# Layer 3 with values projected ahead of the attention, chunk ends in 32x32 blocks on VectorE, output written by columns

## The chip, the cores and the metric

The kernel runs on one core of a Trainium2 chip. The metric is the device time of one execution in microseconds. Another execution, recorded by the hardware profiler, gives the trace from which all durations below come. Lines such as L1281 are lines of the kernel before.

## The reference, cut to what matters

Four attention layers follow each other on four images of 64x64 pixels with 64 channels, all in f32. Only layer 3 changes:

```python
h = group_norm(x, gamma, beta)                    # 8 groups
q = h @ wq + bq;  k = h @ wk + bk;  v = h @ wv + bv
attn = softmax(q k^T / 8) over all 4096 pixels    # (4096, 4096) for each image
proj = (attn v) @ wp + bp
return h + proj
```

Each row of `attn` sums to 1. So `(attn v) @ wp + bp` equals both `(attn h) @ (wv wp) + b` and `attn (h @ (wv wp) + b)`, with b = bv wp + bp. The kernel before computes the first form, the changed kernel the second. The product wv wp lies twice on the diagonal of the 128x128 constant `wv3`, and b in `bv3`.

## The kernel before

An image is held as 128 partitions (two halves of the pixel columns, with 64 channels each) by S = 2048 pixels. Queries are cut into NC = 4 chunks of 512 columns (each for both halves), keys into NB = 32 blocks. A unit u is one chunk with one key block, a step is two units, and a layer takes 64 steps for an image. `attention` (L1231) is shared by layers 2 and 3:

- `first(u)` (L1241): four 64x64 matmuls of 512 columns (L1246) write the scores into a PSUM tile `s`. ScalarE writes their exp to `p` (L1251). VectorE adds `p` to `zacc` (L1257), for the even unit of a step at once, for the odd one at the end of the step, over the list `later`.
- `then(u)`, two steps later: four 64x64 matmuls add `v` times `p` into two PSUM accumulators (L1281).
- When a chunk's keys are through, ScalarE copies one accumulator and VectorE adds the other (L1290, L1291) to give `o`, 128 rows of (half, channel) by 512 pixels. Before that VectorE has turned `zacc` in 32x32 blocks and reduced it to `zsums` (L1265, L1269).
- Two steps later comes `turn(c)` (L1300). In layer 3 four 128x128 matmuls multiply 128 columns of `o` each by `wv3` (L1309), which also turns them, so that pixels are partitions. Four matmuls with `lanes`, a 128x32 constant, sum `zsums` over the lanes (L1229). VectorE copies the sums, takes reciprocals and multiplies (L1312, L1313, L1315).
- Two steps after that comes `last` (L1506). VectorE adds the residual `hb` (L1508), and SyncE issues four DMAs of 64 KB whose rows are the 64 channels of a pixel (L1511).

`before3` (L1443) prepares layer 3 of the next image in the background of the attention that runs: the group norm, the queries (`project`, L884), then sixteen 128x128 transposes of h (L1490) in two groups of eight, each copied by ScalarE to `hT` (L1491), and two adds of the bias on VectorE that give `hb` (L1494). `hT` is the `v` of the attention.

The order of the work is written by hand. `step` (L809) emits, for its two units, `first` for both, `then` for the earlier one, one piece of work from a background generator or the list `urgent` (where `MID` is asked for), then the second `then`, then what lies in `later`. All engines take their instructions in this order. `background(0.6, ...)` gives such a place six times in ten. There are two `s` tiles in PSUM (of two banks each), taken in turn by everything that asks, so a background piece or a `turn` takes one of the two between the scores of two steps. There are 14 `p` tiles, four accumulators, two tiles each of `o` and `turned`, and 13 tiles of 128x2048 in SBUF.

The last chunk of the last image ends in `final` (L1513) instead: in two halves, with a check that all softmax sums were in range (`rest_in_range`, `count_bad`; the result `bad` decides whether a general path runs afterwards). `read_flag` puts a load of `bad` into the queues of all engines (L1826).

Of the kernel before, what the change touches and what calls it, by code (L numbers as in the profile page):

```python
# [8 lines left out]
FP = mybir.dt.float32  # L9
I32 = mybir.dt.int32  # L10
AF = mybir.ActivationFunctionType
ALU = mybir.AluOpType
AX = mybir.AxisListType
# [584 lines left out]
def fast_path(tc: tile.TileContext, a: dict, out: bass.AP, bad, read_flag):  # L598
# [56 lines left out]
    def ctile(shape, name):  # L655
        return const.tile(shape, FP, tag=name, name=name)
# [54 lines left out]
    make_identity(nc, ident)  # L711
    ones = ctile([P, P], "ones")
    nc.gpsimd.memset(ones, 1.0)
    lanes = ctile([P, 32], "lanes")
    nc.vector.tensor_reduce(lanes, ident.rearrange("p (a j) -> p j a", j=32), AX.X, ALU.add)

    def twice(dst, src):
        for i in range(2):
# [26 lines left out]
    rows(gamma0, a["L0_conv_gamma"])  # L745


    NCHECK = B * (NB + 2 + 2 * NC * 8)
    all_z, all_r = ctile([P, NCHECK], "all_z"), ctile([P, NCHECK], "all_r")
    checks = [0]  # L750

# [472 lines left out]
        st["done1"] = True  # L1224


    def add_quarters(z, sums):
        for r in range(4):
            nc.tensor.matmul(z[quarter(r), :], lanes, sums[:, r, :, :], start=True, stop=True)  # L1229

    def attention(st, turned_by, arranged, last, not_before, name, final=None):  # L1231

# [38 lines left out]
        def then(u, within=None):  # L1273
            c, j = divmod(u, NB)
            if j == 0:
                accs[c] = [acc_tile() for _ in range(2)]
            p = ps.pop(u)
            for cols in parts(within, j in (0, NB - 1)):
                for e in range(2):
                    for i in range(2):  # L1280
                        nc.tensor.matmul(  # L1281
                            accs[c][e][half(i), cols], v[half(e), j, :], p[half(e), chunk(i)][:, cols],
                            start=(j == 0), stop=(j == NB - 1),
                        )
            if c == NC - 1 and j == NB - 1 and final is not None:
                final(accs.pop(c), by_query(zsums.pop(c)))
            elif j == NB - 1:
                o = os[c] = o_tile("o")
                acc = accs.pop(c)
                nc.scalar.copy(o, acc[0])  # L1290
                nc.vector.tensor_tensor(o, o, acc[1], ALU.add)  # L1291
                urgent.append((now[0] + 2, lambda: turn(c)))
                urgent.append((now[0] + 4, lambda: last(c, os.pop(c))))
                if c == NC - 1:
                    urgent.append((now[0] + 4, lambda: st.update({name: True})))

        def by_query(sums):
            return sums.rearrange("p (i n r) -> p r n i", i=2, n=4)

        def turn(c):  # L1300


            s = s_tile()
            o, z = s[:, 0:512], s[:, 512 : 512 + 2 * 4]
            for n in range(4):
                if turned_by is ident:
                    nc.tensor.transpose(o[:, ds(n * P, P)], os[c][:, ds(n * P, P)], ident)  # L1307
                else:
                    nc.tensor.matmul(o[:, ds(n * P, P)], os[c][:, ds(n * P, P)], turned_by, start=True, stop=True)  # L1309
            add_quarters(z, by_query(zsums.pop(c)))  # L1310
            z_columns, r_columns = check_columns(2 * 4)
            nc.vector.tensor_copy(z_columns, z)  # L1312
            nc.vector.reciprocal(r_columns, z_columns)  # L1313
            t = os[c] = o_p.tile([P, 2 * 4, C], FP, tag="turned", name="turned")
            nc.vector.tensor_tensor(  # L1315
                t.rearrange(arranged, n=4), o.rearrange("p (n i f) -> p n i f", n=4, i=2),
                r_columns.rearrange("p (n i) -> p n i", n=4).unsqueeze(3).to_broadcast([P, 4, 2, C]), ALU.mult,
            )

        start = now[0]  # L1320
        for t in range(pairs):
# [101 lines left out]
    def layer2(st, not_before):  # L1423
        xv = st["x"].rearrange("p (h g e n) -> p e g n h", h=H, e=2, n=4)

        def last(c, t):
            t = t.rearrange("p (i n) h -> p i n h", i=2)
            s = s_tile()
            for e in range(2):
                for i in range(2):  # L1430
                    nc.tensor.matmul(
                        s[half(i), ds(e * 512, 256)], wp2[half(e), :], t[half(e), i, :, :], start=True, stop=True
                    )
            for e in range(2):
                x_out = xv[:, e, c, :, :]
                nc.vector.scalar_tensor_tensor(
                    x_out, s[:, ds(e * 512, 256)].rearrange("p (n h) -> p n h", h=H), bp2, x_out, ALU.add, ALU.add
                )

        return attention(st, ident, "p (n i) f -> p n i f", last, not_before, "done2")  # L1440


    def before3(on, st):  # L1443
# [38 lines left out]
        st["k"] = h, swapped("h_swapped", h)  # L1482
        st["q"] = x_tile("q")
        yield from project(on, st["q"], blocks[3][0], h, blocks[3][1])
        hT, hb = x_tile("hT"), x_tile("hb")
        for g in range(2):
            yield MID
            s = s_tile()
            for i in range(8):
                nc.tensor.transpose(s[:, ds(i * P, P)], h[:, ds((g * 8 + i) * P, P)], ident)  # L1490
            nc.scalar.copy(hT[:, wide(g)], s)  # L1491
        for g in range(2):
            yield MID
            nc.vector.tensor_tensor(  # L1494
                hb[:, wide(g)].rearrange("p (j f) -> p j f", f=C), hT[:, wide(g)].rearrange("p (j f) -> p j f", f=C),
                bv3.unsqueeze(1).to_broadcast([P, 16, C]), ALU.add,
            )
        st["v"], st["x"] = hT.rearrange("p (j f) -> p j f", f=C), hb

    def layer3(st, not_before):  # L1500


        hb = st.pop("x").rearrange("p (k i f) -> p k i f", i=2, f=C)
        dst = tokens(out[st["b"]])

        def last(c, t):  # L1506
            ks, i = slice(c // 2 * 8, c // 2 * 8 + 8), c % 2
            nc.vector.tensor_tensor(t, t, hb[:, ks, i, :], ALU.add)  # L1508
            for r in range(4):
                queue = nc.scalar if c == NC - 1 and st["b"] == B - 1 and r % 2 else nc.sync  # L1510
                queue.dma_start(dst[r, :, ks, i, :], t[r * W2 : (r + 1) * W2, :, :])  # L1511

        def final(acc, sums):  # L1513

            z = acc_tile()[:, 0:8]
            add_quarters(z, sums)
            z_columns, r_columns = check_columns(8)
            nc.vector.tensor_copy(z_columns, z)
            nc.vector.reciprocal(r_columns, z_columns)
            rest_in_range(z_columns, r_columns)  # L1520
            r_columns = r_columns.rearrange("p (n i) -> p n i", n=4)
            t = o_p.tile([P, 2 * 4, C], FP, tag="turned", name="turned")
            ks = slice((NC - 1) // 2 * 8, (NC - 1) // 2 * 8 + 8)
            turned = []
            for m in range(2):
                o, cols = o_tile("o")[:, 0:256], slice(m * 256, m * 256 + 256)
                nc.scalar.copy(o, acc[0][:, cols])
                nc.vector.tensor_tensor(o, o, acc[1][:, cols], ALU.add)
                s = s_tile()[:, 0:256]
                for n in range(2):  # L1530
                    nc.tensor.matmul(s[:, ds(n * P, P)], o[:, ds(n * P, P)], wv3, start=True, stop=True)
                turned.append(s)
            set_bad = count_bad()
            for m, s in enumerate(turned):
                n = slice(2 * m, 2 * m + 2)
                part = t.rearrange("p (i n) f -> p n i f", n=4)[:, n, :, :]
                nc.vector.tensor_tensor(
                    part, s.rearrange("p (n i f) -> p n i f", n=2, i=2),
                    r_columns[:, n, :].unsqueeze(3).to_broadcast([P, 2, 2, C]), ALU.mult,
                )  # L1540
                nc.vector.tensor_tensor(
                    part, part, hb[:, ks, (NC - 1) % 2, :].rearrange("p (i n) f -> p n i f", n=4)[:, n, :, :], ALU.add
                )
                if m == 0:
                    set_bad()
            flag.append(read_flag())
            for r in range(4):
                queue = nc.scalar if r % 2 else nc.sync
                queue.dma_start(dst[r, :, ks, (NC - 1) % 2, :], t[r * W2 : (r + 1) * W2, :, :])

        return attention(
            st, wv3, "p (i n) f -> p n i f", last, not_before, "done3", final if st["b"] == B - 1 else None
        )


    def alone(*phases):
# [229 lines left out]
    drain()  # L1786


    count = 2 * 4
    in_range, in_range_r, least = ctile([P, count + 2], "in_range"), ctile([P, count], "in_range_r"), ctile([P, 1], "least")  # L1790

    def most_in_range():
# [75 lines left out]
```

## Time and profile before

| what | value |
|---|---|
| median of 3 runs | 2986.95 us (2986.86 to 2987.16) |
| the profiled execution | 2984.41 us |
| its span, first to last instruction | 2982.6 us |
| granted TensorE clock | 0.999 |
| TensorE (PE) busy | 2957.3 us |
| ScalarE (ACT) busy | 1932.2 us |
| VectorE (DVE) busy | 1799.4 us |
| GpSimd (POOL) busy | 34.0 us |
| DMA | 25.79 MB, mean 9 GB/s |

The span lies 1.8 us inside the profiled execution's own time. An f32 matmul is recorded as two instructions, an f32 transpose as one. Lists of instructions show the start and the duration in us, the engine, the line, the operation, the output and inputs, the tile of the array (64\*64 is a quarter of it), the shape, and how many were merged into the row; square brackets show how long the engine had been idle, and for whom it waited. In rows by group, the two numbers behind the bar are the busy time of the group in us and the mean of one in ns.

### The profile page before, as it was taken

How to read it: one execution, taken by the hardware profiler on the slowest of the kernel's cores; microseconds unless marked ns; L12 is line 12 of the kernel's file. 1: busy time of each engine (PE TensorE's matmuls, PEld its weight loads, DVE VectorE, ACT ScalarE, POOL GpSimd, SP SyncE). 2: the span in 40 equal slices, each digit the busy share in tenths (PEclk: the TensorE clock that was granted, in tenths of full speed). 3: DMA queues.
4: the chain of work that ended last, by engine and by line, in shares of the span. 5: the costliest groups of instructions: out<-in, count | busy, mean ns of one | idle time of the engine just before them, and what ended most of it. 6: DMA issues, size and time to landing. Idle time of an engine off the chain costs nothing.

```text
span 2982.6 us, 64616 instructions
## 1 busy us (share of the span) xinstructions
PE 2957.3 (99%) x28485; PEld 1125.8 (38%) x28485; DVE 1799.4 (60%) x2038; ACT 1932.2 (65%) x2777; POOL 34.0 (1%) x32
## 2 busy tenths in 40 slices
PE   9999999999999999999999999999999999999998
PEld 3333233333344433444443333333343334333333
DVE  2211742588721078862027887777877777877777
ACT  6877777665578866567876655555555655555554
POOL 0000000000000000000000000000000000000000
PEclk9999999999999999999999999999999999999999
DMA  2020000000001000000000000000000000000000
GB/s 37 2 30 5 1 2 15 5 1 15 2 1 29 1 5 2 15 1 16 1 1 5 1 16 1 19 5 9 5 19 8 15 1 2 19 5 5 9 5 10
DMA packets 54177, 25.79 MB, mean 9 GB/s; under 512 B 51968, under 2 KB 51968, under 8 KB 52480
## 3 DMA queue, kind: packets, MB, share of 16 engines
q1 hardware_dynamic: 52176, 21.17, 3.9%
q8 instruction: 225, 3.69, 0.5%
q10 hardware_dynamic: 1712, 0.41, 0.1%
q14 instruction: 64, 0.52, 0.1%
HBM read 4.79 MB, written 4.19 MB: 3 GB/s over the span
## 4 chain that ended last, share of the span: by engine, by line
PE 98%; ACT 1%; DVE 1%; issue 0%; DMA 0%; ACTq 0%; DVEq 0%
PE acc L1281 30%; PE s L1246 30%; PE s L987 15%; PE acc L1018 15%; PE s L1111 2%; PE acc L1137 2%; ACT p L1117 1%; PE s L1309 1%; PE s L1137 1%; PE s L903 1%; PE s L1393 0%; PE s L884 0%; PE s L1307 0%; PE s L1490 0%; PE s L1413 0%; PE s L1172 0%
## 5 line engine op out<-in xcount | busy, mean ns | idle before, releaser
L1251 ACT ACTIVATE p<-s 128x1024 f32<-128x1024 f32 x1024 | 994.4, 1022 | 706.4 <-PE s L1246 698.3
L1257 DVE TENSOR_TENSOR zacc<-zacc,p 128x1024 f32<-128x1024 f32 x960 | 1173.8, 1223 | 352.3 <-ACT p L1251 311.5
L1281 PE MATMUL acc<-p,v 64*64 64x512 f32 (+1 forms) x4480 | 517.8, 556 | 0.0
L1018 PE MATMUL acc<-p,vs 64*64 64x512 f32 (+1 forms) x4224 | 512.4, 578 | 0.5 <-ACT vs L1007 0.5
L997 ACT ACTIVATE p<-s 128x1024 f32<-128x1024 f32 x480 | 486.9, 1015 | 34.7 <-PE s L987 15.9
L1281 PE MATMUL acc<-p,hT 64*64 64x512 f32 x4096 | 494.2, 590 | 0.0
L1246 PE MATMUL s<-q,k 64*64 64x512 f32 x2048 | 490.5, 590 | 1.7 <-ACT p L1117 1.7
L987 PE MATMUL s<-xT,q 64*64 64x512 f32 x2048 | 487.9, 591 | 2.5 <-DVE v L904 0.6
L987 PE MATMUL s<-xT,q_swapped 64*64 64x512 f32 x2048 | 488.6, 591 | 0.7 <-DVE o L1146 0.7
L1246 PE MATMUL s<-q,xT 64*64 64x512 f32 x2048 | 486.9, 589 | 0.0
L1246 PE MATMUL s<-q,h_swapped 64*64 64x512 f32 x2048 | 479.3, 589 | 0.0
L1246 PE MATMUL s<-q,k_swapped 64*64 64x512 f32 x2048 | 477.5, 590 | 0.0
L999 DVE TENSOR_REDUCE all_z<-z 128x1 f32<-128x4 f32 x128 | 20.1, 157 | 629.1 <-ACT p L997 628.8
L1281 PEld LDWEIGHTS acc<-p,v 64*64 64x64 f32 x4480 | 175.4, 133 | 295.0 <-issue 292.6
L1018 PEld LDWEIGHTS acc<-p,vs 64*64 64x64 f32 x4224 | 178.7, 133 | 269.2 <-issue 205.5
L1007 ACT ACTIVATE vs<-v,all_r 64x64 f32<-64x64 f32 x512 | 176.7, 345 | 143.4 <-PE acc L1018 71.1
L1281 PEld LDWEIGHTS acc<-p,hT 64*64 64x64 f32 x4096 | 156.7, 133 | 263.8 <-issue 263.1
L987 PEld LDWEIGHTS s<-xT,q_swapped 64*64 64x64 f32 x2048 | 146.1, 133 | 144.0 <-issue 113.7
L987 PEld LDWEIGHTS s<-xT,q 64*64 64x64 f32 x2048 | 147.2, 133 | 135.1 <-issue 105.8
L1246 PEld LDWEIGHTS s<-q,h_swapped 64*64 64x64 f32 x2048 | 144.0, 133 | 141.2 <-issue 135.6
L1246 PEld LDWEIGHTS s<-q,k_swapped 64*64 64x64 f32 x2048 | 144.4, 133 | 139.8 <-issue 98.1
L1246 PEld LDWEIGHTS s<-q,xT 64*64 64x64 f32 x2048 | 143.4, 133 | 140.0 <-issue 137.7
(232 smaller groups left out, 1593.5 us busy)
## 6 DMA issues: line engine op xcount, KB each, us to landing
k_swapped<-k SPq DMA_DIRECT2D x8, 512.0 KB, 5.3
h_swapped<-xT SPq DMA_DIRECT2D x8, 512.0 KB, 5.5
out_dram<-turned SPq DMA_DIRECT2D x62, 64.0 KB, 1.9
xin<-in_x_dram SPq DMA_DIRECT2D x12, 256.0 KB, 6.4
q_swapped<-q SPq DMA_DIRECT2D x6, 512.0 KB, 6.0
pg<-pg SPq DMA_DIRECT2D x8, 128.0 KB, 2.3
xin<-in_x_dram SPq DMA_DIRECT2D x12, 64.0 KB, 2.4
xin<-in_x_dram ACTq DMA_DIRECT2D x4, 64.0 KB, 2.7
```

What stands on the lines that cost most here:

```text
L903: nc.tensor.matmul(s[:, ds(k * P, P)], rhs[:, ds((g * 8 + k) * P, P)], w, start=True, stop=True)
L987: nc.tensor.matmul(s[half(e), chunk(i)], queries(m, i, e), k[half(i), chunk(c)], start=True, stop=True)
L997: nc.scalar.activation(p, s, AF.Exp, accum_out=z)
L1007: nc.scalar.activation(vs[half(e), :], v[half(e), m, :], AF.Copy, scale=rz[half(e), m : m + 1])
L1018: nc.tensor.matmul(acc[c][half(i), cols], vs[half(e), :], ps[2 * t + n][half(e), chunk(i)][:, cols], start=(m == 0 and e == 0), stop=(m == ...
L1111: nc.tensor.matmul(ss[e][half(m), chunk(i)], pgs[0 if e == d else 1][r, ds(n * P + m * C, C)], th[r, chunk(i ^ j)], start=True, stop=True,)
L1117: nc.scalar.activation(pk[e], ss[e], AF.Exp)
L1137: nc.tensor.matmul(acc[quarter(q), :], g[:, k, :], ps[j, k][q // 2][:, chunk(q % 2)], start=(k == 0 or not bank), stop=(k == NK - 1 or not ...
L1246: nc.tensor.matmul(s[half(e), chunk(i)], k[(j + i) % 2][half(i), ds(j // 2 * P + e * C, C)], q[half(i), chunk(c)], start=True, stop=True,)
L1251: nc.scalar.activation(p, s, AF.Exp)
L1257: add = lambda: nc.vector.tensor_tensor(zaccs[c], p0, p, ALU.add)
L1281: nc.tensor.matmul(accs[c][e][half(i), cols], v[half(e), j, :], p[half(e), chunk(i)][:, cols], start=(j == 0), stop=(j == NB - 1),)
```

## The change

In layer 3 the values are projected in the background, and the end of a chunk is reshaped by VectorE's 32x32 block transpose, not by TensorE. `values` (L897), which layer 0 uses too, takes the place of the transposes of h:

```python
def values(v, w, rhs, bias):
    for g in range(2):
        yield MID
        s = s_tile()
        for k in range(8):
            nc.tensor.matmul(s[:, ds(k * P, P)], rhs[:, ds((g * 8 + k) * P, P)], w, start=True, stop=True)
        nc.vector.tensor_tensor(v[...], s.rearrange(...), bias..., ALU.add)
```

`turn` becomes an argument of `attention`. Layer 2's `turn` does what it did (in its matmuls `lanes[:, 0:32]`). `lanes` is twice as wide, by one more copy at the start. In layer 3:

```diff
@@ before3
-        hT, hb = x_tile("hT"), x_tile("hb")
-        for g in range(2):
-            yield MID
-            s = s_tile()
-            for i in range(8):
-                nc.tensor.transpose(s[:, ds(i * P, P)], h[:, ds((g * 8 + i) * P, P)], ident)
-            nc.scalar.copy(hT[:, wide(g)], s)
-        for g in range(2):
-            yield MID
-            nc.vector.tensor_tensor(hb..., hT..., bv3..., ALU.add)
+        st["v"] = x_tile("v").rearrange("p (j f) -> p j f", f=C)
+        yield from values(st["v"], wv3, h, bv3)
@@ layer3
+        h = st.pop("x"), st["k"][1]
+        dst = out[st["b"]].rearrange("(j e b) (i w) (q f) -> j e b i w q f", e=2, b=16, i=2, q=2)
+        def sums(zsums):
+            s = s_tile()
+            for k in range(2):
+                for i in range(2):
+                    nc.tensor.matmul(
+                        s[half(i), ds(k * 512, 16)], lanes[half(k), :], zsums[half(k), i * 16 : i * 16 + 16],
+                        start=True, stop=True,
+                    )
+            z_columns, r_columns = check_columns(16)
+            nc.vector.tensor_reduce(z_columns, s.rearrange("p (k b) -> p b k", k=2)[:, 0:16, :], AX.X, ALU.add)
+            nc.vector.reciprocal(r_columns, z_columns)
+            return z_columns, r_columns
+        def residual(c):
+            t = o_tile("residual")
+            for e in range(2):
+                nc.vector.transpose(t[half(e), :], h[0 if e == c % 2 else 1][half(e), chunk(c // 2 * 2 + e)])
+            return t
+        def divide(t, r):
+            nc.vector.tensor_tensor(blocked(t), blocked(t), r.unsqueeze(2).to_broadcast([P, n, 32]), ALU.mult)
+        def store(c, t, rows, queues):
+            for n in range(4):
+                e, q = divmod(n, 2)
+                queues[n % len(queues)](dst[c // 2, e, rows, c % 2, :, q, :].rearrange("b w f -> w b f"), ...)
+        def turn(o, zsums):
+            t = o_tile("turned")
+            r = sums(zsums)[1]
+            nc.vector.transpose(t, o)
+            divide(t, r)
+            return t
         def last(c, t):
-            nc.vector.tensor_tensor(t, t, hb[:, ks, i, :], ALU.add)
-            for r in range(4):
-                queue.dma_start(dst[r, :, ks, i, :], t[r * W2 : (r + 1) * W2, :, :])
+            nc.vector.tensor_tensor(t, t, residual(c), ALU.add)
+            store(c, t, slice(0, 16), [nc.sync.dma_start])
```

The DMAs' rows are thus 32 channels of a pixel (128 bytes). There are still four of 64 KB for a chunk. `final` now reads, with `kept[0]` the residual of the last chunk, formed eight steps before the layer's end:

```python
def final(acc, zsums):
    z_columns, r_columns = sums(zsums)
    rest_in_range(z_columns, r_columns)
    t = o_tile("turned")
    for m in range(2):
        o, rows, cols = o_tile("o")[:, 0:256], slice(m * 8, m * 8 + 8), slice(m * 256, m * 256 + 256)
        nc.scalar.copy(o, acc[0][:, cols])
        nc.vector.tensor_tensor(o, o, acc[1][:, cols], ALU.add)
        nc.vector.transpose(t[:, cols], o)
        if m == 0:
            set_bad = count_bad()
        divide(t[:, cols], r_columns[:, rows])
        nc.vector.tensor_tensor(t[:, cols], t[:, cols], kept[0][:, cols], ALU.add)
        if m == 0:
            store(NC - 1, t, rows, [nc.sync.dma_start])
            set_bad()
            flag.append(read_flag())
    store(NC - 1, t, slice(8, 16), [nc.sync.dma_start, nc.scalar.dma_start])
```

Before, `read_flag` stood behind the arithmetic of both halves and ahead of the four DMAs.

## The prediction

> **What bounds the kernel now.** I read the page's busy shares and the chain that ended last first.
>
> ```profile
> PE 2957.3 (99%) x28485; PEld 1125.8 (38%) x28485; DVE 1799.4 (60%) x2038; ACT 1932.2 (65%) x2777; POOL 34.0 (1%) x32
> ...
> PE 98%; ACT 1%; DVE 1%; issue 0%; DMA 0%; ACTq 0%; DVEq 0%
> ```
>
> TensorE is busy for 99% of the span and carries 98% of the chain. So a matmul that goes shortens the kernel, provided that no wait comes in its place; work on other engines counts only where TensorE waits for it, or after its last matmul. Next I read TensorE's list over a chunk end of layer 3, from the first row of one group L1281 to the first of the next.
>
> ```profile
> 1885.68 1.90 PE L1281 MATMUL acc<-p,hT 64*64 64x512 f32 x16
> ...
> 1889.12 1.04 PE L1281 MATMUL acc<-p,hT 64*64 64x512 f32 x8
> 1890.09 1.16 PE L1309 MATMUL s<-wv,o 128*128 128x128 f32 x8
> 1891.17 0.25 PE L1229 MATMUL s<-zsums,lanes 128*32 128x8 f32 x8
> 1891.35 1.09 PE L1281 MATMUL acc<-p,hT 64*64 64x512 f32 x8
> ...
> 1893.98 1.90 PE L1281 MATMUL acc<-p,hT 64*64 64x512 f32 x16
> ```
>
> A plain step takes 1889.12 - 1885.68 = 3.44 us; over the whole of layer 3 it is 3.43 or 3.44. The step with a `turn` takes 1893.98 - 1889.12 = 4.86. A chunk end thus costs TensorE 1.43 us: 1.08 from L1309's start to L1229's, 0.18 for the sums, and 0.17 more than the plain 0.86 on either side, where the tile of the array changes. Then the two kinds of background piece that are exchanged, the transposes of h and, in layer 0's preparation, the projection of values:
>
> ```profile
> 1909.43 1.04 PE L1281 MATMUL acc<-p,hT 64*64 64x512 f32 x8
> 1910.40 1.09 PE L1490 MATMUL s<-ident,xT 128*128 128x128 f32 x8
> ...
> 1914.05 1.90 PE L1281 MATMUL acc<-p,hT 64*64 64x512 f32 x16
> ```
>
> ```profile
> 735.06 1.07 PE L1281 MATMUL acc<-p,v 64*64 64x512 f32 x8
> 736.06 2.05 PE L903 MATMUL s<-wv,xT 128*128 128x128 f32 x16
> ...
> 740.66 1.04 PE L1281 MATMUL acc<-p,v 64*64 64x512 f32 x8
> ```
>
> Steps of 4.62 and 5.60: eight transposes cost 1.19 us, eight f32 matmuls of that shape 2.17.
>
> **1. The matmuls of the chunk ends go: -18.5 us.** L1309 has 120 rows, eight to a `turn`, so there are 15 turns (the sixteenth is in `final`). Each loses 1.43 us and gets the new sums, eight instructions of 64x64 with 16 columns, which no row shows. From below they are streaming alone: L1281's eight of 512 columns take 0.86, so 16 columns take 0.03. From above: layer 2's `turn`, four transposes and the same L1229, lengthens its step by 0.93 (4.36); eight transposes take 1911.42 - 1910.40 = 1.02, so half of that leaves 0.42 for sums with the changes of tile. I take 0.20, near L1229's own 0.18 (as many instructions, nearly as few columns), with no change of tile. 15 x (1.43 - 0.20) = 18.5; bounds 15 x 1.01 = 15.2 and 15 x 1.40 = 21.0.
>
> [...]
>
> **2. Values for transposes: +7.8 us.** Two groups for each of four images, 8 x (2.17 - 1.19) = 7.8. ScalarE's copies L1491 (1.01 us) go; VectorE's adds move from SBUF to PSUM and now set the tile `s` free. That add takes 1.23 us (L904). The next step wants this tile 1.72 us after the matmuls (the second half of L1281 and one unit of scores), so it hides while VectorE is less than about 0.4 us late; in the list for layer 0 it waits for TensorE, not TensorE for it. Bounds: 7.0, and 11 if half of the eight are late by one `zacc` add (1.22 - 0.4 = 0.8 each).
>
> **3. VectorE gets 1.9 us more for each chunk end, hidden but for one place: +0.6 us.** Now it spends 0.17 + 0.20 + 0.69 + 0.68 = 1.74 (L1312, L1313, L1315, L1508). Then: reduce 0.19, reciprocal 0.20, transpose 0.62, divide 0.69, two residual transposes, add 0.69. The transpose's row is
>
> ```profile
> L1265 DVE STREAM_TRANSPOSE p<-zacc 128x1024 f32<-128x1024 f32 x32 | 39.8, 1245 | 2.7
> ```
>
> so 512 columns take 0.62. For 64 partitions I take the same 0.62 (if only elements counted, 0.31). Sum 3.63. In a plain step its list shows it idle for 0.88 us, waiting for the exp (L1251), so 1.9 us is worked off in two steps. The odd unit's `zacc` add and its successors queue behind it and come up to 2 us late; they hold only `p` tiles, of which there are 14 for two a step. The sums' tile `s` comes free after the reduce, about a microsecond before it is wanted. TensorE would wait where a background piece that VectorE evicts follows in the step right after `last`. In the order of the program there is one such place, with layer 2's values:
>
> ```profile
> 2189.39 1.23 DVE L1257 TENSOR_TENSOR zacc<-zacc,p 128x1024 f32<-128x1024 f32 x1 [0.41 <-ACT p L1251]
> 2190.53 0.68 DVE L1508 TENSOR_TENSOR turned<-turned,hb 128x512 f32<-128x512 f32 x1
> 2191.13 1.22 DVE L1257 TENSOR_TENSOR zacc<-zacc,p 128x1024 f32<-128x1024 f32 x1
> ```
>
> With 1.93 instead of 0.68, that odd add ends at 2193.8, the next even one at 2195.0, and the evictions L1418 (1.29 together) at 2196.3, where the tile is wanted at about 2195.7: 0.6 us. Bounds 0 and 3 (five such waits, if VectorE runs later than I reckon).
>
> **4. The end, after the last matmul: +1.3 us.** `read_flag` moves ahead of the second half, and the load stands in every queue:
>
> ```profile
> L1826 ACTq TENSOR_LOAD <-bad x1: 472/472/472, 2975.8 to 2975.8; - x1
> ...
> L1826 DVEq TENSOR_LOAD <-bad x1: 539/539/539, 2976.1 to 2976.1; - x1
> ```
>
> ScalarE's second copy and VectorE's second half now wait behind it. From the reciprocal's end at 2973.64 (unmoved): add 0.35, transpose 0.33, `least` (waiting for POOL) until 2974.52, divide 0.42, add 0.43, `bad` 0.13: 2975.5. The load: 2976.0. Copy 0.38, add 0.43, transpose 0.35, divide 0.42, add 0.43: 2978.0, where L1541 now ends at 2976.52: +1.5. SyncE's four DMAs of the first half (about 0.4 each) and its load are over by 2977.4, and hidden. The last DMAs carry half the bytes in as many pieces as now. Their 1024 pieces keep the DMA engines busy for some 1.65 us (2977.4 to 2979.05); half the size takes 0.83 to 1.65. I take 0.2 off: +1.3. Bounds 0.7 and 2.5 (the load as long as two of its rows).
>
> [...]
>
> **At nothing:** the copy of `lanes` at the start (VectorE is idle for 2.20 us before L728; else 0.2); `kept` and the longer range check in the last steps, 1.9 us against 0.88 idle in each of eight steps; the sixteen DMA issues a layer, behind which SyncE only has `h_swapped`, wanted many steps later. An issue takes 0.46 us; were it twice that, SyncE would be busy 4 us in a chunk of 56.
>
> **Sum:** -18.5 + 7.8 + 0.6 + 1.3 = -8.8 us. The profiled execution's 2984.41 becomes 2975.6 (its span 2973.8). It lies 2.5 us under the median of the runs, so from 2986.95 I forecast **2978.2 us**.
>
> **Rivals.** (a) *VectorE becomes the wait, and the kernel is slower.* Its 1.9 us a chunk end would come back as a late release of a tile `s`. If all of it reached TensorE, it would be 15 x 1.9 = 28 us, so 2978.2 + 28 = 3006; it turns the sign from 0.6 us a chunk end on. For it: background evictions do hold TensorE now and then (the step at 2177.79 is 0.22 too long, behind L1398). Against it: the 0.88 idle in each step, and few background pieces near chunk ends. 6%. (b) *The small sums cost what they cost now*, 0.42 with the change of tile: 15 x 0.22 = 3.3 less, 2981.5. For it: eight instructions with their weight loads have a floor, as L1229 shows with 8 columns. Against it: they need no other tile. 14%. (c) *The values' evictions or the end come out at their upper bounds:* +3.2 or +1.2, together 2982.6. 9%. (d) That the change doesn't do what it says: the built program's order has the 16 groups L1309 gone, 16 of 64x16 sums in place of the four-quarter ones, and nothing else moved on TensorE; under 1%.
>
> **The numbers.** The forecast with small deviations, 2975.5 to 2980.5, has 70%. The lower bounds together, -21.0 + 7.0 + 0 + 0.7 = -13.3, give 2973.7; that all fall together is unlikely, and the range stops at 2975.0, with some 5% below it. The high end takes in (b) and (c): 2983.0, with (a) and little else above it. Some 0.2% (6 us) is what a measurement can tell from no change, so faster means under 2981.0: the forecast and part of (b), 77%. Within it: the rest of (b), (c) and a little of (a), 18%. Slower: 5%.
>
> **What would show it.** In TensorE's list a chunk end's step of about 3.63 us, and a step with values of 5.6; the step two after 2190 lengthened by half a microsecond; the last VectorE add's end 5.4 us, not 3.9, behind the end of the last L1281. Wrong it would be if steps of the turn were followed by steps over 3.44 us, with TensorE or its weight loads waiting for VectorE, or if the sums took over 0.4 us.

## The result and the profile after

| what | before | after |
|---|---|---|
| median of 8 runs each | 2986.94 us (2986.23 to 2987.24) | 2977.85 us (2976.6 to 2978.7) |
| the profiled execution | 2984.41 us | 2978.09 us |
| its span | 2982.6 us | 2976.3 us |
| first score matmul of layer 0 begins | 9.91 | 12.83 |
| from there to the end of the last `then` matmul | 2962.68 | 2951.46 |
| from there to the end of the span | 10.02 | 12.01 |

The ratio of the times is 0.9969, with a 95% interval of 0.9958 to 0.998. The changed kernel is 9.1 us faster; 8.8 was forecast. In the changed kernel the scores are L1243, the `then` matmuls L1278, the sums L1493, the values L904, the residual's transposes L1508, the add of `last` L1530, and the load of `bad` L1830.

The page, its first line and the chain by engine:

```profile
PE 2948.0 (99%) x28421; PEld 1126.3 (38%) x28421; DVE 1832.9 (62%) x2088; ACT 1924.7 (65%) x2769; POOL 34.1 (1%) x32
...
PE 97%; ACT 1%; DVE 1%; SPq 0%; issue 0%; DMA 0%; ACTq 0%; DVEq 0%
```

VectorE has 33.5 us more work, TensorE 9.3 less, and TensorE still carries the chain. TensorE's list over a chunk end of layer 3:

```profile
1894.14 1.04 PE L1278 MATMUL acc<-p,v 64*64 64x512 f32 x8
1895.00 0.26 PE L1493 MATMUL s<-zsums,lanes 64*64 64x16 f32 x8
1895.09 1.07 PE L1278 MATMUL acc<-p,v 64*64 64x512 f32 x8
...
1897.69 1.90 PE L1278 MATMUL acc<-p,v 64*64 64x512 f32 x16
```

The four matmuls L1309 are gone. From the first row to the last it is 3.55 us, where it was 4.86, against 3.43 for a plain step. So the sums cost 0.12 us: the next group begins 0.09 behind them, while their own rows last 0.26 beside their neighbours. The same list over values:

```profile
1913.14 1.04 PE L1278 MATMUL acc<-p,v 64*64 64x512 f32 x8
1914.11 2.05 PE L904 MATMUL s<-wv,xT 128*128 128x128 f32 x16
...
1918.72 1.47 PE L1278 MATMUL acc<-p,v 64*64 64x512 f32 x12
```

From the first row to the last it is 5.58 us; with transposes it was 4.62. Taking TensorE's whole list step by step, from one group of scores to the next, in both kernels, only three things differ by more than a tenth of a microsecond, apart from the very first step (0.2, part of the start):

| steps | before | after | together |
|---|---|---|---|
| 15 chunk ends of layer 3 | 4.86 (once 5.09) | 3.55 (once 3.74) | -19.7 us |
| 8 with the background transposes, now values | 4.62 (twice 4.65) | 5.58 (twice 5.61) | +7.7 us |
| two steps after the chunk end at 2178 (at 2186.2 and 2194.0) | 3.43 | 3.53 and 4.11 | +0.8 us |

The sum, -11.2, is that of the first table. With +2.0 at the end that is -9.2, the difference of the medians to a tenth. The +2.0 is that of one pair of executions; ends scatter by more than a microsecond (table of ends below). The profiled executions differ by less, 6.3, because this one reached its first scores 2.9 us later; that part belongs to neither kernel (last section).

### The profile page after: what moved, and what is told of

Same layout as the page of the kernel before. It is cut to its first block, busy times and chain, and to the rows that moved or that the text cites. A ratio compares the mean times of both kernels' runs of the same rounds, so it can differ in the third digit from the quotient of the medians.

```text
span 2976.3 us, 64497 instructions
## 1 busy us (share of the span) xinstructions
PE 2948.0 (99%) x28421; PEld 1126.3 (38%) x28421; DVE 1832.9 (62%) x2088; ACT 1924.7 (65%) x2769; POOL 34.1 (1%) x32
## 4 chain that ended last, share of the span: by engine, by line
PE 97%; ACT 1%; DVE 1%; SPq 0%; issue 0%; DMA 0%; ACTq 0%; DVEq 0%
PE acc L1278 30%; PE s L1243 29%; PE acc L1019 15%; PE s L988 15%; PE s L1112 2%; PE acc L1138 2%; PE s L904 1%; ACT p L1118 1%; PE s L1138 1%; PE s L1367 0%; PE s L885 0%; PE s L1405 0%; PE s L1084 0%; PE s L1173 0%; PE s L1424 0%
## 5 line engine op out<-in xcount | busy, mean ns | idle before, releaser
L1248 ACT ACTIVATE p<-s 128x1024 f32<-128x1024 f32 x1024 | 994.4, 1022 | 709.2 <-PE s L1243 702.7
L1278 PE MATMUL acc<-p,v 64*64 64x512 f32 (+1 forms) x8576 | 1011.0, 572 | 0.0
L1278 PEld LDWEIGHTS acc<-p,v 64*64 64x64 f32 x8576 | 335.1, 133 | 555.2 <-issue 551.5
L998 ACT ACTIVATE p<-s 128x1024 f32<-128x1024 f32 x480 | 487.3, 1015 | 34.6 <-PE s L988 15.8
L1243 PE MATMUL s<-q,k 64*64 64x512 f32 x2048 | 490.5, 590 | 1.7 <-ACT p L1118 1.7
L1243 PE MATMUL s<-q,xT 64*64 64x512 f32 x2048 | 487.7, 589 | 0.0
L1243 PE MATMUL s<-q,h_swapped 64*64 64x512 f32 x2048 | 479.6, 589 | 0.4 <-DVE v L1392 0.4
L1243 PE MATMUL s<-q,k_swapped 64*64 64x512 f32 x2048 | 477.3, 590 | 0.0
L1243 PEld LDWEIGHTS s<-q,h_swapped 64*64 64x64 f32 x2048 | 144.5, 133 | 141.4 <-issue 131.0
L1243 PEld LDWEIGHTS s<-q,k_swapped 64*64 64x64 f32 x2048 | 144.9, 133 | 139.1 <-issue 96.7
L1243 PEld LDWEIGHTS s<-q,xT 64*64 64x64 f32 x2048 | 144.4, 133 | 139.1 <-issue 132.9
L1243 PEld LDWEIGHTS s<-q,k 64*64 64x64 f32 x2048 | 144.9, 133 | 118.8 <-issue 103.1
L1118 ACT ACTIVATE p<-s 128x1024 f32<-128x1024 f32 x128 | 124.2, 1022 | 80.8 <-PE s L1112 80.8
```

Of the source, the lines that this page charges most:

```text
L998: nc.scalar.activation(p, s, AF.Exp, accum_out=z)
L1118: nc.scalar.activation(pk[e], ss[e], AF.Exp)
L1243: nc.tensor.matmul(s[half(e), chunk(i)], k[(j + i) % 2][half(i), ds(j // 2 * P + e * C, C)], q[half(i), chunk(c)], start=True, stop=True,)
L1248: nc.scalar.activation(p, s, AF.Exp)
L1278: nc.tensor.matmul(accs[c][e][half(i), cols], v[half(e), j, :], p[half(e), chunk(i)][:, cols], start=(j == 0), stop=(j == NB - 1),)
```

## The experiments

Nine new kernels were run, one of them twice, and both kernels once more. "Profiled once" is one profiled execution; its time contains the chance of the start, so the steps in its trace are compared. The others were timed in several runs besides, and the number of these is given. Each is a change to the changed kernel unless it says otherwise.

**The sums in the tile of 128 rows** (profiled once).

```diff
-            for k in range(2):
-                for i in range(2):
-                    nc.tensor.matmul(s[half(i), ds(k * 512, 16)], lanes[half(k), :], zsums[half(k), i * 16 : i * 16 + 16], ...)
+            for i in range(2):
+                nc.tensor.matmul(s[half(i), 0:16], lanes, zsums[:, i * 16 : i * 16 + 16], start=True, stop=True)
...
-            nc.vector.tensor_reduce(z_columns, s.rearrange("p (k b) -> p b k", k=2)[:, 0:16, :], AX.X, ALU.add)
+            nc.vector.tensor_copy(z_columns, s[:, 0:16])
```

> The changed kernel with its softmax sums in two matmuls of all 128 rows (128x64 tiles, 4 instructions) in place of four of 64 rows (8 instructions); the result is the same. Theory (a change of the array's tile costs TensorE something of itself): the step of a chunk end gets longer than the 3.55 us it has, to some 3.7, for the 0.17 us that the change of tile cost in the kernel before; 15 steps, +2 us. Rival (only instructions count): half the instructions, so 3.49, -1 us in all.

Measured: 14 of the 15 chunk ends take 3.82 to 3.85 us, the one of 3.74 takes 4.05: +0.27 to +0.30 each, +4.1 in all. The direction is that of the theory, the size twice what was expected; the rival fell. From TensorE's list of this kernel:

```profile
1894.08 1.04 PE L1278 MATMUL acc<-p,v 64*64 64x512 f32 x8
1895.05 0.29 PE L1492 MATMUL s<-zsums,lanes 128*64 128x16 f32 x4
...
1897.90 1.90 PE L1278 MATMUL acc<-p,v 64*64 64x512 f32 x16
```

Half as many instructions cost 0.39 us instead of 0.12: 0.97 passes before they start (0.86 with their neighbours' tile). The price of such small sums is in the other tile, 0.27 us for going there and back. The run doesn't tell a price of the change itself from sums that don't run beside their neighbours because their tile covers both halves of the rows.

**Values alone, in the kernel before** (profiled once): the projected values come in, the chunk ends keep TensorE's shape with transposes in place of L1309.

```diff
-        hT, hb = x_tile("hT"), x_tile("hb")
...
+        hT = x_tile("hT")
+        st["v"], st["x"] = hT.rearrange("p (j f) -> p j f", f=C), hT
+        yield from values(st["v"], wv3, h, bv3)
...
-                    nc.tensor.matmul(s[:, ds(n * P, P)], o[:, ds(n * P, P)], wv3, start=True, stop=True)
+                    nc.tensor.transpose(s[:, ds(n * P, P)], o[:, ds(n * P, P)], ident)
```

> The kernel before with the values projected in the background and chunk ends on TensorE, four transposes in place of the four products with wv3. It leaves out the residual (the projected values are added in its place), so VectorE's two adds that make hb are gone too. Theory (the two terms on TensorE's list nearly cancel without the move to VectorE): steps with a chunk end 4.36 instead of 4.86, eight steps of 5.57 instead of 4.62, so 15 x -0.50 + 8 x 0.96 = +0.2 us up to the last L1281, and the time about the one before. Rival (the gain comes from projecting the values early, not from taking the reshaping off TensorE): the time is near the changed kernel's, 9 us less.

Measured: the chunk ends 4.86 to 4.36, the eight steps 4.62 to 5.58; from first scores to last matmul 2962.80, before 2962.68. So 15 x 0.50 = 7.5 is given back as 7.7, and half the change brings nothing. The rival fell. The other 0.81 of each chunk end, 12.2 us, comes from the reshaping on VectorE: by the chunk ends of the experiment before (3.82, with sums in another tile), some 0.54 of it is the transposes that go, and 0.27 the sums that can then stay in their neighbours' tile.

**h not projected** (profiled once): transposes of h in place of the values, and all else as changed.

```diff
-        st["v"] = x_tile("v").rearrange("p (j f) -> p j f", f=C)
-        yield from values(st["v"], wv3, h, bv3)
+        hT = x_tile("v")
+        for g in range(2):
+            yield MID
+            s = s_tile()
+            for i in range(8):
+                nc.tensor.transpose(s[:, ds(i * P, P)], h[:, ds((g * 8 + i) * P, P)], ident)
+            nc.scalar.copy(hT[:, wide(g)], s)
+        st["v"] = hT.rearrange("p (j f) -> p j f", f=C)
```

> The changed kernel with the projection of the values undone: h is transposed by TensorE and copied by ScalarE as in the kernel before, and the attention averages h. It leaves out the product with wv wp and the bias, in the output too. Theory (the projected values cost TensorE 0.98 us for each of eight groups): the eight steps of 5.57 to 5.61 us become 4.62, 7.7 us less up to the last L1278, and all other steps stay. Rival (VectorE's evictions of the values cost something as well): more than 8.5 us less, and steps after those of the values get shorter.

Measured: just the eight steps shrink, by 0.96 each, together 7.7 us, as expected; 2968.08 in all, with an early start. No other step moves by more than a tenth, but for the one at the start. The evictions by VectorE had added nothing.

**The residual formed twice** (profiled once): 1.4 us more of VectorE's work at each chunk end.

```diff
         def last(c, t):
+            residual(c)
             nc.vector.tensor_tensor(t, t, residual(c), ALU.add)
```

> The changed kernel with the two residual transposes of each chunk end done twice (1.4 us more of VectorE for each of 15 chunk ends). Theory (VectorE's work at a chunk end is hidden, but for the one place where layer 2's values follow in the next step): the step that is 4.11 now grows to between 5.0 and 5.6, and all others stay, so +1 to +1.5 us. Rival (VectorE is close to being the bound): each chunk end costs more, up to 15 x 1.4 = 21 us.

Measured: +3.9 us up to the last matmul, in four places: 1.39 at 2081.5, 0.41 at 2159.9, 1.44 at 2196.0, 0.57 at 2315.6. The other chunk ends hide the 1.4 whole; if none were hidden, it would be 21. The first place on VectorE:

```profile
2078.34 5.20 DVE L1254 TENSOR_TENSOR zacc<-zacc,p 128x1024 f32<-128x1024 f32 x4
2083.46 0.18 DVE L1318 COPY mean<-s 128x32 f32<-128x32 f32 x1
```

and on TensorE:

```profile
2083.70 0.65 PE L1243 MATMUL s<-q,h_swapped 64*64 64x512 f32 x2 [1.16 <-DVE mean L1318]
```

In the changed kernel the same four `zacc` adds stand ahead of this copy:

```profile
2076.76 5.21 DVE L1254 TENSOR_TENSOR zacc<-zacc,p 128x1024 f32<-128x1024 f32 x4
2081.88 0.18 DVE L1318 COPY mean<-s 128x32 f32<-128x32 f32 x1
```

In both kernels VectorE goes from `last` to the copy with gaps of at most 0.1 us, so the 1.4 us more come through whole. In the changed kernel the copy ended at 2082.06, some 0.2 us before the scores that want its tile (2082.24). The cover holds at quiet chunk ends; where a background piece waits for VectorE it is nearly used up. The step that took 4.11 grew to 5.55, as expected; that all others stay, and with it the +1 to +1.5 us, fell, and so did the rival's 21.

**The flag load behind both halves** (profiled once).

```diff
                 if m == 0:
                     store(NC - 1, t, rows, [nc.sync.dma_start])
                     set_bad()
-                    flag.append(read_flag())
+            flag.append(read_flag())
             store(NC - 1, t, slice(8, 16), [nc.sync.dma_start, nc.scalar.dma_start])
```

> The changed kernel with the load of the range flag put behind the arithmetic of both halves of the last chunk, as it was. Theory (the load in ScalarE's and VectorE's queue holds up the second half): the last VectorE add ends 4.6 to 4.8 us behind the last L1278 instead of 5.8, and ScalarE's second copy follows the first at once. What of it the span shows is bounded by SyncE, whose four DMAs of the first half last until 3.1 us after they begin: its last two start 0.5 us earlier than now, so the stretch from the last L1278 to the end goes from 12.0 to between 10.9 and 11.5. Rival (the end is longer because of the transposes and small pieces, not the load): no change of that stretch beyond 0.3.

Measured: VectorE's last add ends 4.73 us after the last matmul instead of 5.81, as expected; but the end stays, at 12.06 us, and half of the expectation fell. SyncE's last store begins 7.07 us after the last matmul, in the changed kernel 7.05. The next four take up that queue.

**The flag late, and the residual formed early**, at the tenth step of each chunk (8 runs).

```diff
-            nc.vector.tensor_tensor(t, t, residual(c), ALU.add)
+            nc.vector.tensor_tensor(t, t, kept.pop(c), ALU.add)
...
+        for c in range(NC):
+            before.setdefault(now[0] + c * NB // 2 + 9, []).append(
+                lambda c=c: later.append(lambda: kept.update({c: residual(c)}))
+            )
```

> The changed kernel with the flag's load behind both halves, and the residual of each chunk transposed nine steps after the chunk's first step, not in the step of its last add. Theory: the step of 4.11 becomes 3.43 and the one of 3.53 before it stays, -0.7 us; the end gives what the late flag gives, -0.5 to -1.1; together 1.2 to 1.8 us under the changed kernel in the same rounds. Rival (the residual's work elsewhere holds up other evictions): steps between the chunk ends get longer than 3.44 and take it back.

Measured: a median of 2977.3 us (8 runs, 2973.4 to 2979.6), a ratio of 0.9966 (0.9955 to 0.9976), no different from the changed kernel. The step at 2194 lost its 0.67, and 0.58 came back in two steps from 1864.6 on. There ScalarE and TensorE show

```profile
1866.42 1.06 ACT L1457 ACTIVATE sq<-xT 128x1024 f32<-128x1024 f32 x1 [1.63 <-DVE xT L1455]
```

```profile
1868.53 0.65 PE L1243 MATMUL s<-q,xT 64*64 64x512 f32 x2 [0.32 <-ACT p L1248]
```

The residual now delays a piece of layer 3's group norm on VectorE (L1455); ScalarE waits for it, with the exps queued behind it, and TensorE for an exp. The wait was moved, as the rival said. The end of the profiled execution was 1.1 us shorter than the changed kernel's (table below), as expected of the late flag; with the flag late alone it was not, and the two lie within the scatter of ends, so no gain is shown.

**The first half's stores on both queues**: with the flag late (8 runs), and alone (profiled once).

```diff
-                    store(NC - 1, t, rows, [nc.sync.dma_start])
+                    store(NC - 1, t, rows, [nc.sync.dma_start, nc.scalar.dma_start])
```

> The changed kernel with the flag load behind both halves and with the first half's four stores shared between SyncE and ScalarE, as the second half's are. Theory: in the changed kernel, and with the flag late, the end is set by SyncE's own queue: its four stores of the first half, one of which took 1.5 us to issue, and its flag load, so that its last two stores could begin only 6.7 us after the last matmul, whether VectorE's last add ended at 5.8 or at 4.7. With two stores instead of four ahead of it, SyncE is free by then: the last add at about 4.7 us, the last stores begun at 4.8 to 5.2 on both queues, and the stretch from last matmul to end 10.0 to 10.6 us (12.0 in the changed kernel, 12.05 with the flag late alone); the time about 1.5 us under the changed kernel's, 2976 us in median. Rival: the long issue belongs to the number of stores in flight, not to the queue; then an issue of about 1.5 us comes on one of the two queues as well, the last stores begin no sooner than 6 us and the stretch stays at 11.5 to 12.5. The stretch of one kernel scatters by some 0.9 us from run to run.

> The changed kernel with the first half's four stores shared between SyncE and ScalarE, the flag load where the change has it. Theory: SyncE's queue is free in time, but ScalarE's second copy now stands behind two stores (0.8 us) and the flag load, so VectorE's last add ends at about 6.5 us after the last matmul instead of 5.8, and the last stores begin at 6.6, no sooner than now (6.7): the stretch to the end stays at about 12 (11 to 12.8 with its scatter). Rival: the queue of SyncE alone sets the end, whatever VectorE does: then 10.5 to 11.

**One store of both halves, the flag late** (profiled once, then 6 runs).

```diff
                 if m == 0:
-                    store(NC - 1, t, rows, [nc.sync.dma_start])
                     set_bad()
-                    flag.append(read_flag())
+            flag.append(read_flag())
-            store(NC - 1, t, slice(8, 16), [nc.sync.dma_start, nc.scalar.dma_start])
+            store(NC - 1, t, slice(0, 16), [nc.sync.dma_start, nc.scalar.dma_start])
```

> The changed kernel with no early store of the first half: the four stores carry both halves and stand behind the last add, two on SyncE and two on ScalarE, as in the kernel before, and the flag load behind both halves. Theory: the last add ends at about 4.6 us after the last matmul, all four stores begin behind it at 4.7 to 5.2, and from there it is as in the kernel before, where 6.1 us passed from the last add to the end: a stretch of 10.7 us, 1.3 less than the changed kernel, so that the early half store brings nothing here. Rival: rows of 128 bytes, twice as many pieces for the same bytes as before, make the last transfers longer by up to 1.7 us: 11.5 to 12.4.

> The same kernel as in the one look at a single store with the flag late, timed in rounds. Theory: the end is 1.3 to 1.5 us shorter than the changed kernel's, whose runs so far had medians of 2977.9 and 2977.4: a median of 2976.2, a ratio to the kernel before of 0.9964, and in the profile again a stretch of 10.2 to 11.2 us from the last matmul to the end. Rival: the 10.5 of the one look was scatter; then a stretch of about 12 and 2977.6. The kernel's runs fall into two groups some 2.8 us apart by when TensorE gets its clock at the start, so the median can be off by a microsecond either way; the stretch decides.

Measured, in us after the end of the last matmul:

| kernel | last add ends | last store begins | last store lands | end of the span |
|---|---|---|---|---|
| before | 3.93 | 4.46 | 8.64 | 10.02 |
| before, another execution | 3.93 | 4.46 | 8.44 | 9.83 |
| changed | 5.81 | 7.05 | 10.34 | 12.01 |
| changed, another execution | 5.81 | 7.52 | 11.10 | 12.76 |
| changed, residual twice | 5.81 | 6.47 | 9.35 | 11.02 |
| flag late | 4.73 | 7.07 | 10.40 | 12.06 |
| flag late, residual early | 4.73 | 6.81 | 9.20 | 10.86 |
| flag late, first half on both queues | 6.12 | 6.57 | 10.19 | 11.95 |
| first half on both queues alone | 6.69 | 7.14 | 10.71 | 12.47 |
| flag late, one store | 4.73 | 5.43 | 9.10 | 10.55 |
| flag late, one store, again | 4.73 | 5.42 | 9.22 | 10.67 |

The end follows the landing of the last store by 1.4 to 1.8 us, and within 0.02 by the same for one arrangement of the stores: 1.38 in the kernel before, 1.66 with four early stores on SyncE. (Landings are those that the profile records.) What scatters is the time of that landing: 2.4 to 3.6 us after the last store begins with four early stores on SyncE, 4.0 and 4.2 in the kernel before. The end never follows the last add alone: with the flag late the add is 1.1 earlier, but not the last store. With both queues and the flag late, the last add came at 6.12, not 4.7: I had overlooked that ScalarE's second copy now stands behind its two stores, which the chain of this kernel shows:

```profile
2967.65 0.34 ACTq L1518
...
2968.03 0.46 ACTq L1518
...
2968.54 0.38 ACT o L1540
```

So its expectation fell. The end lies where the rival had it, but not for the rival's reason, since no early issue on the two queues took over 0.5. Its median is 2978.2 us (8 runs, ratio 0.9972, 0.9962 to 0.9983). Sharing the stores alone went as expected: the add at 6.69, and no gain. Only without the early half is the last store more than 0.6 us earlier, by 1.6, and the end by 1.3 to 1.5 with it, as expected. Timed, that kernel has a median of 2976.79 us (6 runs, 2973.77 to 2977.01) and a ratio of 0.9965 (0.9953 to 0.9977). Its two ends, 10.55 and 10.67, lie below the three of the changed kernel's end in the table (11.02 to 12.76) and those of the same end in the first and the third experiment (11.91 and 12.62), though not far below the lowest; the intervals of the times overlap, so in the times alone a gain over the changed kernel is not shown.

**Both kernels once more**: the kernel before (profiled once) and the changed kernel (6 runs).

> The kernel before, unchanged, for another look at its first 20 us. In the profile of the changed kernel the same first matmuls ran at half speed for longer (16 of L885 in 3.69 us, against 1.95), which put everything 3.15 us later. Theory (this is chance of the moment at which the clock is released, and belongs to neither kernel): the first score matmul starts at either about 9.9 or about 12.8 us, in this kernel too. Rival (the change delays the start): 9.9 here, 12.8 in all kernels with the wider lanes.

> The changed kernel again, timed in five rounds, and for another look at its first 20 us. Theory: 2976.5 to 2978.7 us, 9 us under the kernel before; the first score matmul at either 9.9 or 12.8 us. Rival (the change delays the start): at 12.8.

Measured: the kernel before took 2987.12 us, with its first scores at 12.68 and not at 9.91, and 2962.89 from there to its last matmul, as before. The changed kernel had a median of 2977.41 us (6 runs), a ratio of 0.9967 (0.9955 to 0.998), its first scores at 12.99, and 2951.93 over the same stretch. Both theories held, and the rival, that the change delays the start, fell.

## Why the prediction was right, and where its steps were off

**What bounds the kernel** held: TensorE's list accounts for the change to a tenth of a microsecond, and 33.5 us more on VectorE show in 0.8.

**1. The chunk ends: -18.5 forecast, -19.7 measured.** The term that was mis-sized is the sums: 0.20 taken, 0.12 measured. The 0.20 was an estimate, without the 0.17 of the change of tile, and no row of the kernel before shows such sums. I had likened them to L1229's 0.18, whose rows stand in another tile (128\*32) than their neighbours; within the neighbours' tile the next group begins 0.09 us after the sums, whose rows last 0.26. That the tile, not the number of instructions, is the price was shown by the sums in 128 rows: 0.39 us with four instructions, 0.12 with eight. Rival (b), 0.42, fell for the kernel as it is; with another tile the sums cost 0.39, close to it.

**2. The values: +7.8 forecast, +7.7 measured**, and confirmed by taking them out (-7.7) and by adding them alone (+7.7).

**3. VectorE: +0.6 forecast, +0.8 measured, at the place named.** VectorE's list, then TensorE's:

```profile
2189.59 0.70 DVE L1508 STREAM_TRANSPOSE residual<-h_swapped 64x512 f32<-64x512 f32 x1
2190.30 0.71 DVE L1508 STREAM_TRANSPOSE residual<-xT 64x512 f32<-64x512 f32 x1
2191.04 0.69 DVE L1530 TENSOR_TENSOR turned<-turned,residual 128x512 f32<-128x512 f32 x1
2191.65 2.55 DVE L1254 TENSOR_TENSOR zacc<-zacc,p 128x1024 f32<-128x1024 f32 x2
2194.12 1.28 DVE L1392 TENSOR_TENSOR v<-s,bv 128x512 f32<-128x512 f32 x2
```

```profile
2195.54 0.65 PE L1243 MATMUL s<-q,h_swapped 64*64 64x512 f32 x2 [0.45 <-DVE v L1392]
```

The evictions of layer 2's values stand behind the odd and the even `zacc` add, as reckoned, and TensorE waits for them. From the start of this step they end 1.37 us in (2195.40 - 2194.03), where 1.41 was forecast (2196.3 - 2194.89), by two small errors that cancel: from its own rows the odd add would have ended at 2193.7, not 2193.8 (2190.53 + 1.93 + 1.22), while each transpose took 0.70 and not 0.62. VectorE's work at a chunk end is 2.2 us more than before (0.18 + 0.25 + 0.70 + 0.69 + 1.41 + 0.69 = 3.92, against 1.74), not 1.9. Rival (a), VectorE as the wait, fell, but its limit is nearer than I thought: another 1.4 us a chunk end, 3.6 in all, cost 3.9 us, and then the kernel's gain would have been 5.2, not 9.1.

**4. The end: +1.3 forecast, +2.0 measured. This step was wrong in its parts.** The chain that ended last shows ScalarE's copy behind the flag load, as said:

```profile
2967.24 0.07 DVE bad L1813
...
2967.33 0.47 ACTq L1830
...
2967.88 0.38 ACT o L1540
...
2968.29 0.43 DVE o L1541
```

The last add came 5.81 us after the last matmul, not 5.4: the load ended 0.1 later than reckoned, and the five operations behind it took 2.30 with their gaps, not 2.01. "SyncE's four DMAs of the first half and its load are over by 2977.4, and hidden" failed. On SyncE the fourth store took long to issue, and the flag load and the last stores came behind it:

```profile
2968.80 1.52 SPq L1518 DMA_DIRECT2D out_dram<-turned  x1
...
2970.98 0.82 SPq L1518 DMA_DIRECT2D out_dram<-turned  x2
```

```profile
L1830 SPq TENSOR_LOAD <-bad x1: 485/485/485, 2970.4 to 2970.4; - x1
```

By the kernel before's 0.4 a store and its 0.5 for the load, SyncE would have been free some 0.2 us before the end of the last add (2970.98 less the 1.06 that the one store took beyond 0.46, against 2970.11); as it was, it was free 0.9 behind it. So the last store began 2.59 us later than before: 1.88 from VectorE, 0.71 from SyncE's queue. It landed after 3.29 us instead of 4.18, and from there to the end passed 1.66 instead of 1.38: together a gain of 0.6 where I took 0.2. By the records of their packets, a packet of 128 bytes took 13.5 ns and one of 256 took 22.5 (means of the stores between 1800 and 2950 us), so half the bytes in as many packets took 0.60 of the time. Of the 1.65 us that would leave an estimated 0.99, where the sum had 1.45. Errors of opposite sign left the term 0.7 off, and part of this is chance: the five ends of this kind without the late flag, 11.02 to 12.76, lie 1.0 to 2.9 above the kernel before's 9.83 and 10.02.

**Together:** the chunk ends gave 1.2 more than reckoned, the values cost 0.1 less, the stall 0.2 and the end 0.7 more, which leaves 0.4 more gain than the 8.8; the medians show 0.3 more. That the sum came out closer than its terms is luck. So is the step from the profile to the median, 2.5 us, which was right without a known reason; the late start of other executions (2.8 us) accounts for it.

## What to carry to other kernels

Where one engine is busy throughout, reckon a change in that engine's list, step by step, and ask of every other engine only what stands queued behind the added work and who waits for it. Look at the tile of small operations too: here eight small instructions in the tile of their neighbours cost 0.12 us, four in another tile 0.39. At the end of a kernel follow each queue to its last store, and that store to its landing: an early store, or a load in the middle, helps only if nothing that ends last stands behind it in any queue (here the changed kernel and its variants ended 10.86 to 12.76 us after the last matmul with the early stores, and 10.55 and 10.67 without them).

## What the runs showed of the hardware

**VectorE's 32x32 transposes of 512 columns took as long on 64 partitions, 702 ns, as on 128, 696.** A group of the changed kernel, with its mean in ns:

```profile
L1508 DVE STREAM_TRANSPOSE residual<-xT 64x512 f32<-64x512 f32 x16 | 11.2, 702 | 0.1
```

128x512 takes 696 ns (L1525), 128x1024 1245, 128x256 446: not in proportion, and more than the 620 that I had halved from the 1245.

**The start differs from execution to execution.** The same sixteen matmuls in the kernel before:

```profile
7.96 1.95 PE L884 MATMUL acc<-xT,A 64*64 64x512 f32 x16
```

and in another execution of the same kernel:

```profile
9.52 3.34 PE L884 MATMUL acc<-xT,A 64*64 64x512 f32 x16
```

The first scores begin at 9.9 us in three of the profiles, and at 12.4 to 13.0 in the others, over both kernels and all variants. The runs of the kernel before agree with it: most lie between 2986 and 2988, some at 2983.6 to 2984. The granted clock differs: in the traces of the first table, the record of the full clock begins 5.21 us into the span in the kernel before and 12.93 us in the changed kernel, whose first scores begin at 9.91 and 12.83. (The profile's mean clock reads 1.00 ahead of it as well, where no record stands.) The matmuls go with it: two instructions of L703 take 1.22 us from 3.85 or 3.86 on in both, but 0.70 from 7.33 on in the kernel before, and still 1.22 from 8.21 on in the changed one. Groups of four of the sixteen start 0.43 to 0.48 us apart in the kernel before, 0.85 to 0.91 in the changed one. What decides when the full clock comes is not shown.

**A store's issue sometimes took far longer than its usual 0.32 to 0.46 us:** in all seven profiles with four early stores on SyncE (five in the table, and the first and the third experiment), the fourth took 0.9 to 2.0 us. Shared between two queues, none of the early ones took over 0.5, but late stores took up to 1.0 us there and up to 1.6 in other profiles. Why is open.
